# Second sequence's input rows in the first attention: squares turned by VectorE and moved by DMA in place of TensorE transposes

## The chip, the core and the metric

The kernel runs on one core of one Trainium2 chip. The metric is the device time of one execution in microseconds (us), as the median of several runs. A profile is one execution recorded by the hardware; its times are counted from the start of its span.

## The reference, cut to what matters

Two layers, each an attention and a gated feed-forward block with residual and layer norm, on an input x of 2 sequences of 512 rows of 512 numbers, all float32. The change lies in the first attention:

```
q   = x @ Wq.T + bq                    # only 8 of 32 heads of 128 are used
sig = elu(q) + 1
num = einsum('bshd,hde->bshe', sig, M) ;  den = einsum('bshd,hd->bsh', sig, z) + 1e-6
x   = layernorm(x + repeat(num / den, 4 heads) @ Wo.T)
```

The keys and values of this attention do not enter the output, so the kernel leaves them out. The feed-forward block that follows takes weights that are meant to have three values (-s, 0, s); the kernel checks this at run time and has two ways to go on.

## The kernel before, in words

All matmuls contract over the 128 partitions, so x must stand transposed: features on partitions, rows along the free axis. For each of the 2 sequences the first attention keeps such a copy, `xt_a00` and `xt_a01`, 128 x 4 x 512 numbers: four blocks k of 128 features for 512 rows. `query_products` (L323) makes one head of one sequence: four matmuls, one per block k, add up into one PSUM buffer of 128 x 512. `queries` (L352) then has ScalarE compute e = exp (L361) and r = relu (L363) from PSUM, and VectorE q = min(e, 1) + r (L365). The tiles e and r have two buffers each, q has sixteen. There are eight PSUM buffers in all, taken in turn.

The loops stand at L453 to L493. The first sequence's heads 0 to 7 run first. `first_rows` transposes that sequence's rows tile by tile for head 0, so that work starts as rows arrive. In the loop, after head 4, `sum_weights` adds up groups of output weights and `turn_memory` transposes m; after head 6 `transposed(xs[1], "a01")` (L115) makes the second sequence's copy: 16 TensorE transposes (L125) of 128 x 128 into four PSUM buffers, two ScalarE copies and two VectorE copies into `xt_a01` (L127). On TensorE they come to stand before head 7. Then the second sequence's heads follow. Between them stand `fold` (output weights multiplied into m, giving `mw`), and, for the ternary check, `largest` (L177, VectorE: the greatest weight of the first gate/up chunk), `over_partitions` (L184, a TensorE transpose) and `scales` (L195 to L199), which give `inv_up`. From the second sequence's head 3 on, `check_up` has ScalarE divide gate/up chunks by the scale (L433) and VectorE compare them (L204). After that `read` (L392) multiplies the queries by `mw` and adds the result to x.

The order on each engine is set by a scheduling layer from program order and expected readiness, except where `tc.issue_after(step)` ties a step behind another; GpSimd keeps the program's order. Each engine works through its own list in order, and a waiting instruction holds up all behind it. Loads are issued from SyncE's list (SP), a few from ScalarE's; each issue is itself an instruction there. A load signals its landing through one of eight completion semaphores, which loads of both lists take in turn; an issue waits until the load that last used its semaphore has landed.

Loads in order: x of the first sequence, query weights `wq`, x of the second sequence (four tiles `x_1_0` to `x_1_3`, L89), `m`, then 16 output weight tiles `wo` (two per head, L305, pool of six buffers, so that later ones wait for `sum_weights` of earlier ones, L380 and L382), with the first gate/up chunk `gu0` ahead of head 6's, the other ten chunks (L237, 512 KB each), and small weights of the second layer.

`mw` is 128 x 8 x 512; its last column holds z (L321, GpSimd).

Of the kernel before, what the change touches and what calls it, by code (L numbers as in the profile page):

```python
# [10 lines left out]
F32 = mybir.dt.float32  # L11
# [3 lines left out]
AF = mybir.ActivationFunctionType  # L15
ALU = mybir.AluOpType
# [3 lines left out]
P = 128  # L20
B, S, HID = 2, 512, 512
NT = S // P
NK = HID // P
NH, G, D = 8, 4, 128
INTER = 1376
CHUNKS = [(i, min(P, INTER - i)) for i in range(0, INTER, P)]
GROUPS = [4, 4, 3]
LN_EPS = 1e-5
DEN_EPS = 1e-6
LAST = HID - 1  # L30
LENT = 3
TOP12 = -4096
BELOW_HALF = 0.5 - 2.0**-13
# [3 lines left out]
def kernel(  # L37
# [19 lines left out]
    nc = tc.nc  # L57
# [6 lines left out]
    xtp = ctx.enter_context(tc.tile_pool(name="xtp", bufs=2))  # L64
# [7 lines left out]
    wqkv = const.tile([P, NK, 3 * D], F32, tag="wqkv", name="wqkv")  # L72
    bv = const.tile([P, D], F32, tag="bv", name="bv")
    wo1 = const.tile([D, HID], F32, tag="wo1", name="wo1")
    bo = const.tile([P, HID], F32, tag="bo", name="bo")
# [3 lines left out]
    def psum(name):  # L79
        return ps.tile([P, 512], F32, tag="mm", name=name)  # L80


    xs = [[], []]
# [9 lines left out]
    bq = const.tile([D, NH], F32, tag="bq", name="bq")  # L93
    z = const.tile([D, NH], F32, tag="z", name="z")
# [20 lines left out]
    def transposed(rows, name, in_turn=False):  # L115

        xt = xtp.tile([P, NK, S], F32, tag="xt", name=f"xt_{name}")
        done = None
        for k in range(NK):
            pt = psum(f"pt_{name}_{k}")  # L120
            with ExitStack() as tied:
                if in_turn and k:
                    tied.enter_context(tc.issue_after(done.ins))
                for t in range(NT):
                    done = nc.tensor.transpose(pt[:, ts(t, P)], rows[t][:, ts(k, P)], ident)  # L125
            move = nc.vector.tensor_copy if k == 1 or k % 2 > in_turn else nc.scalar.copy
            copies.append(move(xt[:, k, :], pt))  # L127
        return xt
# [43 lines left out]
    def largest(blocks, name):  # L172

        k = len(blocks)
        mx = small.tile([P, k], F32, tag=f"mx{k}", name=f"mx_{name}", bufs=1)
        for i, w in enumerate(blocks):
            nc.vector.reduce_max(mx[:, i : i + 1], w, AX.X)  # L177
        return mx
# [52 lines left out]
    def up_weights(gu_in, name, chunks=range(len(CHUNKS))):  # L231
        gus = []
        for c in chunks:
            i, n = CHUNKS[c]
            gu = wffn.tile([P, 2, NK, n], F32, tag=f"gu{c}", name=f"gu{name}_{c}")
            at = 2 * HID * i
            nc.sync.dma_start(  # L237
                gu.rearrange("p a k i -> p (a k i)"),
                gu_in[at : at + 2 * HID * n].rearrange("(p f) -> p f", p=P),
            )  # L240
            gus.append(gu)
        return gus
# [38 lines left out]
    with tc.tile_pool(name="a0w", bufs=1) as a0w, tc.tile_pool(name="a0", bufs=2) as a0:  # L281
        wq = []
# [16 lines left out]
        for h in range(NH):  # L299
            halves = []  # L300
            if h == 6:
                gus = up_weights(gu0_in, "0", range(1))
# [3 lines left out]
                halves.append(w)  # L306
            wos.append(halves)

        gus += up_weights(gu0_in, "0", range(1, len(CHUNKS)))
        nc.sync.dma_start(wqkv, wqkv_in.rearrange("(k p) f -> p k f", p=P))  # L310
        bqk = const.tile([D, 3], F32, tag="bqk", name="bqk")
        nc.sync.dma_start(bqk, bqk_in)
        nc.sync.dma_start(bv, bv_in.to_broadcast([P, D]))
        nc.sync.dma_start(wo1, wo1_in)
        nc.sync.dma_start(bo, bo_in.to_broadcast([P, HID]))

        mw = a0w.tile([D, NH, HID], F32, tag="mw", name="mw")  # L320
        nc.gpsimd.tensor_copy(mw[:, :, LAST], z)  # L321

        def query_products(pq, xt, h, at):  # L323
            for k in range(NK):
                done = nc.tensor.matmul(  # L325
                    pq[:, at], wq[h][:, k, :], xt[:, k, at],
                    start=(k == 0), stop=(k == NK - 1),
                )
            return done

        def first_rows(xt, t):

            pt = psum(f"pt_a00_{t}")
            for k in range(NK):
                done = nc.tensor.transpose(pt[:, ts(k, P)], xs[0][t][:, ts(k, P)], ident)
            pt = pt.rearrange("p (k t) -> p k t", k=NK)
            nc.scalar.copy(xt[:, :2, ts(t, P)], pt[:, :2])
            nc.vector.tensor_copy(xt[:, 2:, ts(t, P)], pt[:, 2:])
            return done

        def first_queries(pq, xt):
# [7 lines left out]
                    done = query_products(pq, xt, 0, ts(t, P))  # L349
            return done  # L350

        def queries(b, xt, h):  # L352

            pq = psum(f"pq_{b}_{h}")
            if b == h == 0:
                done = first_queries(pq, xt)
            else:
                done = query_products(pq, xt, h, slice(0, S))

            e = a0.tile([D, S], F32, tag="e", name=f"e_{b}_{h}")  # L360
            nc.scalar.activation(e, pq, AF.Exp, bias=bq[:, h : h + 1])  # L361
            r = a0.tile([D, S], F32, tag="r", name=f"r_{b}_{h}")
            nc.scalar.activation(r, pq, AF.Relu, bias=bq[:, h : h + 1])  # L363
            q = a0.tile([D, S], F32, tag="q", name=f"q_{b}_{h}", bufs=16)
            nc.vector.scalar_tensor_tensor(q, e, 1.0, r, ALU.min, ALU.add)  # L365
            qs[b].append(q)
            return done

# [8 lines left out]
        def sum_weights(eng, h):  # L377

            w, w1 = wos[h]
            eng.tensor_add(w, w, w1)  # L380
            s = a0.tile([D, HID], F32, tag="wos", name=f"wos{h}", bufs=4)
            eng.tensor_add(s, w[:, 0, :], w[:, 1, :])  # L382
            wos[h] = s

        def fold(h):
            p = psum(f"pmw_{h}")
            nc.tensor.matmul(p, m[:, h, :], wos[h], start=True, stop=True)
            c = small.tile([P, 1], F32, tag="col", name=f"col_{h}", bufs=2)
            nc.scalar.mul(c, p[:, LAST:], -1.0)
            nc.scalar.activation(mw[:, h, :LAST], p[:, :LAST], AF.Identity, bias=c)  # L390

        def read(b, t, between):  # L392
# [3 lines left out]
            for h0 in range(0, NH, 4):  # L396
                four = []
                den = small.tile([P, 4], F32, tag="den", name=f"den_{b}_{t}_{h0}")
                for j in range(4):
# [5 lines left out]
                    nc.scalar.activation(  # L405
                        den[:, j : j + 1], po[:, LAST:], AF.Identity, bias=den_eps
                    )
                    four.append(po)
                nc.vector.reciprocal(den, den)
                for j in range(4):  # L410
                    d = den[:, j : j + 1]
                    if h0 + j < LENT:
                        y = a0.tile([P, HID], F32, tag="y", name=f"y_{b}_{t}_{j}", bufs=3)
                        nc.scalar.activation(  # L414
                            y[:, :LAST], four[j][:, :LAST], AF.Copy, scale=d
                        )
                        if ys:
                            nc.gpsimd.tensor_add(  # L418
                                ys[0][:, :LAST], ys[0][:, :LAST], y[:, :LAST]
                            )  # L420
# [32 lines left out]
        xt = xtp.tile([P, NK, S], F32, tag="xt", name="xt_a00")  # L453
        with tc.issue_after(queries(0, xt, 0).ins):
            queries(0, xt, 1)
        for h in range(2, NH):
            queries(0, xt, h)
            if h == 4:
                sum_weights(nc.gpsimd, 0)
                turn_memory()  # L460
                sum_weights(nc.vector, 1)
            elif h == 6:
                xt1 = transposed(xs[1], "a01")
                sum_weights(nc.vector, 2)
        sum_weights(nc.gpsimd, 3)
        for h in range(NH):
            queries(1, xt1, h)
            if h == 0:
                sum_weights(nc.vector, 4)
                sum_weights(nc.gpsimd, 5)  # L470
                fold(0)
                fold(1)
                mx_up = largest(
                    [gus[0][:, a].rearrange("p k i -> p (k i)") for a in range(2)], "up"
                )
            elif h == 1:
                top_up = over_partitions(mx_up, "up")
            elif h == 2:
                sc_up, inv_up = scales(top_up, "up")
                fold(2)  # L480
                fold(3)
                sum_weights(nc.vector, 6)
                sum_weights(nc.gpsimd, 7)
            elif h == 3:
                fold(4)
            elif h == 5:
                fold(5)
                fold(6)
            elif h == 6:
                fold(7)  # L490
            if h >= 3:
                for _ in range(3):
                    check_up(*checks.pop(0))  # L493
# [250 lines left out]
    gus = up_weights(gu1_in, "1", range(6, len(CHUNKS) - 1))  # L744
    gus.append(joined_weights(gu1_in, len(CHUNKS) - 1))
    wds = down_weights(wd1_in, "1")
    gus = up_weights(gu1_in, "1", range(6)) + gus
# [91 lines left out]
    for b in range(B):  # L839
# [5 lines left out]
        xt = xt_a1[b]  # L845
# [4 lines left out]
        for j in range(2):  # L850
            p = psum(f"pqk_{b}_{j}")
# [11 lines left out]
        for t in range(NT):  # L863
            p = psum(f"pv_{b}_{t}")
# [167 lines left out]
    t = NT - 1  # L1032
# [248 lines left out]
```

## Time and profile before

| what | value |
|---|---|
| median of 3 runs | 471.82 us (471.29 to 472.02) |
| the profiled execution's own time | 471.99 us |
| its span | 470.0 us |
| mean granted TensorE clock | 0.996 |
| TensorE busy | 463.0 us (99%) |
| VectorE, ScalarE, GpSimd busy | 327.9, 268.1, 114.4 us |
| DMA | 33.97 MB, mean 72 GB/s |
| small DMA packets | 3440 under 512 B, of 15187 |

How to read it: busy time is the sum over an engine's instructions. A matmul that waits for its PSUM buffer or for its operand can be shown as a long matmul, so a busy TensorE isn't TensorE at its peak. The page also has the span in 40 equal slices (each digit is the busy share in tenths), the chain of work that ended last, and groups of instructions by line. In the timeline an entry has its start, its duration, engine, line, output and inputs, and in brackets the idle time before it and what ended it. Names have their buffer numbers left out: `xt_a` is any of the two copies, `pt_a` a PSUM buffer of transposes.

The chain that ended last runs through TensorE for 72% of the span, ScalarE for 7% and VectorE for 5%. Between 54.9 and about 118 us it runs through ScalarE and VectorE, before and after mainly through TensorE.

### The profile page before, as it was taken

The numbers are of one execution on the slowest core, as the hardware profiler recorded it, in microseconds if no ns is written. First come the engines' busy times: TensorE is split into PE (matmuls) and PEld (weight loads), VectorE is DVE, ScalarE is ACT, GpSimd is POOL, SyncE is SP. The second block draws the span as 40 slices with busy tenths as digits, with TensorE's granted clock in tenths as the row PEclk, the third lists the DMA queues.
The fourth block names the chain that finished last, engine by engine and source line by source line (L and its number), as shares of the span: only waits on it lengthen the run. The fifth ranks groups of instructions, "written<-read, shape, count | busy, mean of one in ns | idle before, by whom it ended". The sixth has DMA issues, their size and how long they took to land.

```text
span 470.0 us, 5725 instructions
## 1 busy us (share of the span) xinstructions
PE 463.0 (99%) x1899; PEld 330.7 (70%) x1899; DVE 327.9 (70%) x622; ACT 268.1 (57%) x507; POOL 114.4 (24%) x141
## 2 busy tenths in 40 slices
PE   9999999999999999999999999999999999999995
PEld 8454444434478788888866568888888888888885
DVE  1265677767857677755988989986666767998633
ACT  3344799557556877645756743575644768532201
POOL 0343101566460090400348032000000000041101
PEclk9999999999999999999999999999999999999998
DMA  8999800000015000213192000000000000001011
GB/s 311 373 348 382 301 2 0 0 0 3 1 54 188 3 1 1 92 47 81 58 360 94 0 1 1 1 0 1 1 0 1 0 1 1 1 24 45 22 46 45
DMA packets 15187, 33.97 MB, mean 72 GB/s; under 512 B 3440, under 2 KB 4336, under 8 KB 15152
## 3 DMA queue, kind: packets, MB, share of 16 engines
q1 hardware_dynamic: 14864, 33.14, 19.6%
q8 instruction: 22, 0.36, 0.3%
q10 hardware_dynamic: 288, 0.36, 0.2%
q14 instruction: 13, 0.11, 0.1%
HBM read 31.40 MB, written 2.10 MB: 71 GB/s over the span
## 4 chain that ended last, share of the span: by engine, by line
PE 72%; ACT 7%; DVE 5%; issue 3%; POOL 0%; POOLq 0%; DVEq 0%; ACTq 0%
PE pm L1071 17%; PE pg_f L567 9%; PE pu_f L567 8%; PE pc L1071 8%; PE pdm L1159 7%; PE pd_f L622 4%; PE pdc L1159 4%; DVE x L423 4%; PE pqk L853 3%; PE po L401 2%; ACT y L414 2%; ACT t L433 2%; PE pv L866 2%; PE pot L949 1%; PE po L965 1%
## 5 line engine op out<-in xcount | busy, mean ns | idle before, releaser
L401 PE MATMUL po<-mw,q 128*128 128x512 f32 x128 | 57.1, 598 | 0.3 <-DVE mv_a L137 0.2
L325 PE MATMUL pq<-xt_a,wq 128*128 128x512 f32 (+1 forms) x152 | 56.9, 526 | 0.0
L143 POOL TENSOR_TENSOR rstd_f<-mv_f,ln_eps 128x1 f32<-128x1 f32 x15 | 4.4, 295 | 172.1 <-DVE mv_f L1174 130.2
L401 PEld LDWEIGHTS po<-mw,q 128*128 128x128 f32 x128 | 23.0, 189 | 32.1 <-issue 17.7
L325 PEld LDWEIGHTS pq<-xt_a,wq 128*128 128x128 f32 x152 | 26.2, 190 | 27.3 <-issue 26.2
L1071 PE MATMUL pm<-r,ugu 128*128 128x512 f32 x152 | 37.7, 389 | 0.0
L1071 PE MATMUL pm<-r,it_early 128*128 128x512 f32 x144 | 36.7, 392 | 0.0
L1071 PEld LDWEIGHTS pm<-r,ugu 128*128 128x128 f32 x152 | 28.5, 188 | 5.9
L1071 PEld LDWEIGHTS pm<-r,it_early 128*128 128x128 f32 x144 | 27.0, 188 | 6.0 <-issue 0.5
L423 DVE SCALAR_TENSOR_TENSOR x<-po,den,x 128x511 f32<-128x511 f32 x40 | 29.8, 745 | 1.9
L165 ACT ACTIVATE ta_f<-y_f,below_half 128x512 int8<-128x512 f32 (+1 forms) x22 | 15.9, 723 | 23.7 <-DVE y_f L155 23.3
L1081 DVE SCALAR_TENSOR_TENSOR ev_q<-pm,ev_q 128x512 f32<-128x512 f32 x27 | 18.6, 687 | 14.1 <-PE pm L1071 14.1
L418 POOL TENSOR_TENSOR y<-y,y 128x511 f32<-128x511 f32 x16 | 20.3, 1272 | 31.5 <-ACT y L414 30.8
L593 DVE SCALAR_TENSOR_TENSOR it_f<-tb_f,ta_f 128x512 fp32r<-128x512 int16 (+1 forms) x22 | 15.2, 690 | 16.3 <-ACT tb_f L166 16.3
L361 ACT ACTIVATE e<-pq,bq 128x512 f32<-128x512 f32 x16 | 11.1, 691 | 24.1 <-PE pq L325 21.7
L567 PE MATMUL pg_f<-xh,tu 128*128 128x512 f32 x88 | 24.7, 401 | 0.0
L1080 ACT ACTIVATE ev_q<-pc 128x512 f32<-128x512 f32 x27 | 16.0, 594 | 14.1 <-PE pc L1071 14.0
L435 POOL TENSOR_SCALAR td<-wd,inv_down 128x512 fp32r<-128x512 f32 x11 | 18.6, 1710 | 22.0 <-DVE inv_down L199 22.0
L567 PE MATMUL pg_f<-xl,tu 128*128 128x512 f32 x88 | 23.6, 390 | 0.0
L567 PE MATMUL pu_f<-xh,tu 128*128 128x512 f32 x88 | 23.6, 389 | 0.0
L567 PE MATMUL pu_f<-xl,tu 128*128 128x512 f32 x88 | 23.5, 389 | 0.0
L961 ACT ACTIVATE x<-x,off_f,rstd_f 128x512 f32<-128x512 f32 x7 | 5.7, 816 | 27.7 <-POOL off_f L960 27.7
(310 smaller groups left out, 1088.3 us busy)
## 6 DMA issues: line engine op xcount, KB each, us to landing
gu<-in_gu SPq DMA_DIRECT2D x20, 512.0 KB, 8.0
wo<-in_wo SPq DMA_DIRECT2D x16, 512.0 KB, 5.7
wd<-in_wd SPq DMA_DIRECT2D x20, 256.0 KB, 4.9
wq<-in_wq SPq DMA_DIRECT2D x8, 256.0 KB, 4.1
x<-in_x SPq DMA_DIRECT2D x7, 256.0 KB, 4.4
out<-x SPq DMA_DIRECT2D x7, 256.0 KB, 2.0
wqkv<-in_wqkv SPq DMA_DIRECT2D x1, 768.0 KB, 10.7
m<-in_m SPq DMA_DIRECT2D x1, 512.0 KB, 5.8
```

Of the source, the lines that this page charges most:

```text
L165: nc.scalar.activation(a[:n], y, AF.Relu, bias=below_half[:n])
L325: done = nc.tensor.matmul(pq[:, at], wq[h][:, k, :], xt[:, k, at], start=(k == 0), stop=(k == NK - 1),)
L401: nc.tensor.matmul(po, qs[b][h0 + j][:, ts(t, P)], mw[:, h0 + j, :], start=True, stop=True,)
L418: nc.gpsimd.tensor_add(ys[0][:, :LAST], ys[0][:, :LAST], y[:, :LAST])
L423: steps.append(nc.vector.scalar_tensor_tensor(x[:, :LAST], four[j][:, :LAST], d, x[:, :LAST], ALU.mult, ALU.add))
L435: eng.tensor_scalar(out, w, factor, None, ALU.mult)
L567: nc.tensor.matmul(pp[a], t[:, a, i % NK, :], x2[b][i], start=(i == 0), stop=(i == 2 * NK - 1),)
L622: nc.tensor.matmul(pd, inter[b][c][:, ts(t, P)], td[c].bitcast(F32R), start=(c == 0), stop=(c == last),)
L1071: nc.tensor.matmul(p, w, x, start=(left[id(p)] == begun[id(p)]), stop=(left[id(p)] == 1))
L1080: nc.scalar.activation(ev, pc, AF.Copy, scale=CROSS)
L1081: nc.vector.scalar_tensor_tensor(ev, pm, MAIN, ev, ALU.mult, ALU.add)
L1159: nc.tensor.matmul(p[:, :w], got[j // 4][1][kind][:, j % 4], down_parts[j][kind][:, cols], start=(j == 0 and kind == kinds[0]), stop=(j == ...
```

## The change

The 16 transposes and four copies are gone. `xt_a01` has another layout, 128 x 4 x 4 x 128: tile of rows t, block k, row within the tile. VectorE transposes each of the four tiles of the second sequence's rows in squares of 32 x 32 that stay where they are (`turn_squares`) into the first half of `mw`, which isn't needed yet. The squares are then brought to their places by DMA: 16 transfers inside SBUF on ScalarE's list (`move_squares`), each from 32 partitions to 32 partitions with 16 runs of 32 numbers (128 bytes) per partition, 64 KB in all. The VectorE squares are tied behind q of the first sequence's head 0, and two groups of eight transfers behind r of heads 1 and 2. `query_products` reads the second sequence as four runs of 128 columns. As `mw` is lent out, z is written to it only after the second sequence's head 0. `largest` is tied behind q of the first sequence's head 6. The loads from the second gate/up chunk on are issued from a function that is called later in the program.

```diff
+SQ = 32
-        gus += up_weights(gu0_in, "0", range(1, len(CHUNKS)))
-        nc.sync.dma_start(wqkv, wqkv_in.rearrange("(k p) f -> p k f", p=P))
...
+        def later_loads():
+            gus.extend(up_weights(gu0_in, "0", range(1, len(CHUNKS))))
+            nc.sync.dma_start(wqkv, wqkv_in.rearrange("(k p) f -> p k f", p=P))
...
         mw = a0w.tile([D, NH, HID], F32, tag="mw", name="mw")
-        nc.gpsimd.tensor_copy(mw[:, :, LAST], z)
...
+                rows = xt[:, :, k, :] if xt is xt1 else xt[:, k, at]
                 done = nc.tensor.matmul(
-                    pq[:, at], wq[h][:, k, :], xt[:, k, at],
+                    pq[:, at], wq[h][:, k, :], rows,
...
+        xt1 = xtp.tile([P, NT, NK, P], F32, tag="xt", name="xt_a01")
+        squares = mw[:, :NT, :]
+
+        def turn_squares(t):
+            nc.vector.transpose(squares[:, t, :], xs[1][t])
+
+        def move_squares(i):
+
+            src = squares.rearrange("p t (k i) -> p (t k) i", k=NK)
+            dst = xt1.rearrange("p t k i -> p (t k) i")
+            for j in range(P // SQ):
+                nc.scalar.dma_start(dst[ts(j, SQ), :, ts(i, SQ)], src[ts(i, SQ), :, ts(j, SQ)])
...
+        relus, elus = [], []
...
-            nc.scalar.activation(r, pq, AF.Relu, bias=bq[:, h : h + 1])
+            relus.append(nc.scalar.activation(r, pq, AF.Relu, bias=bq[:, h : h + 1]))
-            nc.vector.scalar_tensor_tensor(q, e, 1.0, r, ALU.min, ALU.add)
+            elus.append(nc.vector.scalar_tensor_tensor(q, e, 1.0, r, ALU.min, ALU.add))
...
         for h in range(2, NH):
             queries(0, xt, h)
+            if h == 2:
+                with tc.issue_after(elus[0].ins):
+                    for t in range(NT):
+                        turn_squares(t)
+            if h < 4:
+                with tc.issue_after(relus[h - 1].ins):
+                    for i in range(2):
+                        move_squares(2 * h - 4 + i)
...
             elif h == 6:
-                xt1 = transposed(xs[1], "a01")
                 sum_weights(nc.vector, 2)
         sum_weights(nc.gpsimd, 3)
+        later_loads()
         for h in range(NH):
             queries(1, xt1, h)
             if h == 0:
+                nc.gpsimd.tensor_copy(mw[:, :, LAST], z)
...
-                mx_up = largest(
-                    [gus[0][:, a].rearrange("p k i -> p (k i)") for a in range(2)], "up"
-                )
+                with tc.issue_after(elus[6].ins):
+                    mx_up = largest(
+                        [gus[0][:, a].rearrange("p k i -> p (k i)") for a in range(2)], "up"
+                    )
```

More of the change, by code (lines that the diff above doesn't have):

```diff
@@ L307 @@
             wos.append(halves)
-        gus += up_weights(gu0_in, "0", range(1, len(CHUNKS)))
-        nc.sync.dma_start(wqkv, wqkv_in.rearrange("(k p) f -> p k f", p=P))
         bqk = const.tile([D, 3], F32, tag="bqk", name="bqk")
[L312 to L315, printed above, removed]
+        def later_loads():
+            gus.extend(up_weights(gu0_in, "0", range(1, len(CHUNKS))))
+            nc.sync.dma_start(wqkv, wqkv_in.rearrange("(k p) f -> p k f", p=P))
+            nc.sync.dma_start(bqk, bqk_in)
+            nc.sync.dma_start(bv, bv_in.to_broadcast([P, D]))
+            nc.sync.dma_start(wo1, wo1_in)
+            nc.sync.dma_start(bo, bo_in.to_broadcast([P, HID]))
         mw = a0w.tile([D, NH, HID], F32, tag="mw", name="mw")
-        nc.gpsimd.tensor_copy(mw[:, :, LAST], z)
         def query_products(pq, xt, h, at):
             for k in range(NK):
+                rows = xt[:, :, k, :] if xt is xt1 else xt[:, k, at]
                 done = nc.tensor.matmul(
-                    pq[:, at], wq[h][:, k, :], xt[:, k, at],
+                    pq[:, at], wq[h][:, k, :], rows,
                     start=(k == 0), stop=(k == NK - 1),
```

## The prediction

> **What bounds the kernel now.** I read the 40 slices of the page, then the timeline of the first 50 us, then busy time by stage, then the DMA views.
>
> The slices (11.75 us each) have TensorE busy throughout, and the DMA engines full for the first five:
>
> ```profile
> PE   9999999999999999999999999999999999999995
> DMA  8999800000015000213192000000000000001011
> GB/s 311 373 348 382 301 2 0 0 0 3 1 54 188 3 1 1 92 47 81 58 360 94 0 1 1 1 0 1 1 0 1 0 1 1 1 24 45 22 46 45
> ```
>
> The timeline around the edited step (start, duration, engine, line, idle time before it):
>
> ```profile
> 30.53 5.82 SPq L305 DMA_DIRECT2D wo<-in_wo  x4
> ...
> 32.18 1.91 PE L125 MATMUL pt_a<-ident,x 128*128 128x128 f32 x16
> ...
> 33.93 7.03 PE L325 MATMUL pq<-xt_a,wq 128*128 128x512 f32 x16
> ...
> 34.75 1.28 DVE L177 TENSOR_REDUCE mx_up<-gu 128x1 f32<-128x512 f32 x2 [1.23 <-DMA gu<-in_gu]
> ...
> 37.56 0.69 ACT L361 ACTIVATE e<-pq,bq 128x512 f32<-128x512 f32 x1 [2.95 <-PE pq L325]
> 37.75 1.21 DVE L380 TENSOR_TENSOR wo<-wo,wo 128x1024 f32<-128x1024 f32 x1
> ...
> 45.95 0.27 PE L184 MATMUL pmx_up<-ident,mx_up 128*2 128x128 f32 x1
> ```
>
> Here TensorE sets the pace: a head takes 7.03 / 2 = 3.5 us, ScalarE and VectorE wait for it, and 16 transposes stand between two heads. Head 7 of the first sequence runs from 33.93, so the second sequence's first head starts at about 37.4; it is the first reader of xt_a01. From 54 us ScalarE is full, so TensorE's "busy" there is mostly waiting for PSUM:
>
> ```profile
> 46.00:54.00 8.00, 8.00 (x22) 3.64 (x21) 4.46 (x9) 5.15 (x10) 2.03 (x2) 1.00 1.03 402
> 54.00:75.00 21.00, 21.00 (x51) 9.28 (x50) 14.82 (x38) 20.78 (x40) 0.00 (x0) 1.00 0.11 37
> ```
>
> (columns: stretch, length, then busy time and instructions of PE, PEld, DVE, ACT, POOL, clock, DMA share, GB/s). ScalarE's weight checks (L433) need inv_up, which comes from TensorE's L184 and L195. So a delay of TensorE before 50 us moves all that follows, one to one; so does a gain, if L184 moves too.
>
> The DMA view of 20 to 40 us, then that of 219 to 226 us, where three loads have rows of 384, 128 and 256 bytes:
>
> ```profile
> DMA packets 1864, 6.79 MB, mean 340 GB/s; under 512 B 206, under 2 KB 206, under 8 KB 1864
> q1 hardware_dynamic: 1864, 6.79, 93.8%
> wo<-in_wo SPq DMA_DIRECT2D x10, 512.0 KB, 5.5
> ```
>
> ```profile
> DMA packets 1585, 0.41 MB, mean 59 GB/s; under 512 B 1584, under 2 KB 1584, under 8 KB 1584
> q1 hardware_dynamic: 1584, 0.39, 27.1%
> gu<-in_gu SPq DMA_DIRECT2D x1, 192.0 KB, 2.7
> gu<-in_gu SPq DMA_DIRECT2D x1, 64.0 KB, 3.9
> ```
>
> The stretch that receives the 16 moves is 94% full. A small packet costs 0.271 x 16 x 7 us / 1584 = 19 ns[...], a 4 KB one, at 400 GB/s over 16 engines, 163 ns.
>
> [...]
>
> **The change, part by part.**
>
> *Removed.* 16 transposes: 33.93 - 32.18 = 1.75 us of TensorE, on the path. Two ScalarE copies (1.07 us) and two VectorE copies (2 x 0.68), both in idle time: worth nothing. TensorE now wants xt_a01 at 37.4 - 1.75 = 35.6.
>
> *VectorE squares.* Four 128x512 transposes; the nearest row, a 128x512 copy, takes 0.68[...]. x_1_3 is issued at 9.0 and lands 5.0 later. VectorE is idle from 12.9 (query 0 of head 0)[...]; I take 15.6, when ScalarE finishes r of head 1 and can issue.
>
> *ScalarE's 16 issues.* 0.41 us is its one such row, 0.51 that of the 512-row load on SyncE: 8 us in all. ScalarE idles 2.17 us per head here, so this alone would be hidden.
>
> *The waits of those issues* decide. The built program has eight completion semaphores, which loads of both queues take in turn, and an issue waits until the last load with its semaphore has landed. Moves 3 to 6 wait for wo0's second, wo1's second, and wo2's two loads; moves 7 to 16 each wait for the move four earlier. The last is at the end of the chain wo1 -> move 4 -> 8 -> 12 -> 16. VectorE's add of wo1 starts at 21.90 in the trace, on its landing: move 4 goes out at 22 at the earliest. Four links then give the arrival of xt_a01: 22 + 4 x link.
>
> *One link.* A lone move of 512 packets takes at least 2.7 and at most 3.9 us to land by the two rows above; I take 3.2, of which 512 x 19 ns / 16 = 0.6 is data. Beside queued weights each engine has 32 rows of a move to serve in turn with 4 KB rows. If a turn is one row: 32 x (163 + 19) ns = 5.8, a link of 3.2 - 0.6 + 5.8 = 8.4 us.[...] I take 7.6[...]. Arrival: 22 + 30.4 = 52.4; bounds 45.2 and 55.6, and 34.8 if no turn is ever lost.
>
> *Cost on the path.* The first head of the second sequence starts at 52.4 instead of 37.4: +15.0, transposes already counted. TensorE has been idle since 35.6[...].
>
> *What is queued behind.* On ScalarE, e and r of heads 3 to 7 and two copies of m stand among and behind the moves: 5 x 1.37 + 1.07 = 7.9 us. Move 16 goes out at 44.8, so they are done by 52.7, before the next head ends at 55.8. TensorE meanwhile fills PSUM buffers of heads 3 to 7 and m, seven of eight: no stall from that. On SyncE, the two loads of wo4 take the semaphores of moves 1 and 2, and three later gate/up chunks those of moves 13 to 15: weights come later, but their readers are later too. On GpSimd, the copy of z into mw waits for the moves that read it and holds the sums of heads 5 and 7, read late in the second sequence: nothing. later_loads swaps one SyncE load: nothing. Reading xt_a01 as four runs of 128 columns: no row shows it. Four separate 128-column matmuls would cost 36 ns more each (8 of them took 1.17 us at 6.14, against 438 / 4 ns), 9 us over 64 matmul records; one instruction has no such restarts and those after 54 us lie under ScalarE's work: I take nothing, bound 3 us before 54.
>
> Sum: +15.0 + 1.7 = 16.7 on the profiled execution's 471.99 us (span 470.0 and 2.0 around it): 488.7; that execution is 0.17 above the median of 471.82. Forecast 488.5.
>
> **Rivals.**
>
> *Moves pass quickly; the maximum is late.* If links cost 3.2 to 3.9, xt_a01 is there at 35 to 38. Then L177 is next: it now stands after head 6's q, and VectorE's order puts the wo6 sum (37.75 in the trace) ahead of q of head 4, which e of head 6 needs, since e has two buffers. Some 12 of the moves, 12 x 0.6 = 7 us of DMA work, come ahead of wo6 and push it from about 37 to 44; then the sum 1.2, q 0.7, e and r 1.4, q 0.7 and L177's 1.3 end at 49, against 45.95 for L184: +3, 475; up to 481 with double the packet cost. For it: transfers inside SBUF may be cheap. Against: the full queue.
>
> *Packets inside SBUF are dearer*, 60 ns: 31 us of all engines, over 500.
>
> *Faster.* Decides if xt_a01 lands before 35.6 and L177 ends before 45.95 - 1.75 = 44.2: then the transposes are pure gain, 470.1. It needs every link under 3.4 us in a stretch that is 94% full, and weights hardly delayed.
>
> **How the numbers follow.** Crawling moves 0.54 (482 to 494: arrival 45.2 to 55.6[...]); quick moves and late maximum 0.30 (474 to 481); dear packets 0.06; no change 0.04; faster 0.06. A measurement of this kernel tells about 0.2% from none. Range 474 to 496: it leaves out the last three cases, and a little of the first. Faster 0.06, same 0.04, slower 0.90.
>
> **What would show it.** Right: TensorE idle before its first second-sequence head, ended by DMA xt_a; to-landing times of moves of 5 us and more while weights are queued; ScalarE idle before moves 7 to 16 on DMA xt_a; the clock below 1 just after the gap. Wrong: moves that land within 3.5 us, TensorE's wait ended by mx_up or by no DMA, or a later stage that gives the delay back.

## The result, and the profile after

The changed kernel takes 490.34 us (median of 6 runs, 489.27 to 492.93) against 471.63 us before in the same session: a ratio of 1.0391, 95% interval 1.0375 to 1.0407. The forecast was 488.5 in a range of 474 to 496. The profiled execution is the slowest of the six (492.93 us, span 490.7), so the profile shows about 2.6 us more than a typical run.

The slices of the page, now 12.27 us each:

```profile
PE   9980399999999999999999999999999999999995
...
PEclk9995599999999999999999999999999999999999
DMA  8999920000000600022229000000000000001011
```

TensorE, busy throughout before, has a hole in slices 3 to 5, its granted clock is at half there (0.50 from 39.0 to 59.5 us), and the DMA engines are busy into a sixth slice (five before). The timeline of that stretch (entries that end in `q` are issues of transfers, standing in that engine's list):

```profile
12.74 2.85 DVE L338 STREAM_TRANSPOSE mw<-x 128x512 f32<-128x512 f32 x4 [0.18 <-DMA x<-in_x]
...
15.62 1.49 ACTq L345 DMA_DIRECT2D xt_a<-mw  x2
...
31.54 14.39 ACTq L345 DMA_DIRECT2D xt_a<-mw  x7
...
46.03 0.69 ACT L379 ACTIVATE e<-pq,bq 128x512 f32<-128x512 f32 x1 [14.69 <-DMA xt_a<-mw]
...
52.43 0.68 DVE L178 TENSOR_REDUCE mx_up<-gu 128x1 f32<-128x512 f32 x1
...
56.58 5.11 PE L328 MATMUL pq<-xt_a,wq 128*128 128x512 f32 x8 [21.14 <-DMA xt_a<-mw]
...
63.25 3.60 PE L328 MATMUL pq<-xt_a,wq 128*128 128x512 f32 x8
```

The squares are ready at 15.6 us. The 16 moves leave ScalarE between 15.6 and 45.1; ScalarE itself stands still behind them, once for 11.3 us and once for 14.7. TensorE has nothing left from 35.4 on and starts the second sequence's first head at 56.58 in place of 37.4. That head takes 5.11 us, a later one 3.60. The maximum (L178) is finished 3.5 us before TensorE starts: it isn't what TensorE waits for.

Busy time by stage (columns as in the prediction):

```profile
35.50:56.50 21.00, 0.00 (x0) 0.00 (x0) 5.09 (x7) 5.71 (x10) 0.15 (x1) 0.58 1.04 330
...
75.00:96.00 21.00, 21.00 (x50) 9.31 (x49) 14.93 (x37) 20.85 (x40) 0.00 (x0) 1.00 0.00 0
```

The second line is the stage with ScalarE full, which stood at 54 to 75 before, with 20.78 us of ScalarE then and 20.85 now. Nothing is given back: the delay of the first head, 56.58 - 37.4 = 19.2, and 1.5 us of slow clock (5.11 - 3.60) make 20.7, and this execution is 492.93 - 471.99 = 20.9 longer.

The DMA view of 15 to 60 us (packets, MB, share of the engines; q1 is SyncE's queue, q10 ScalarE's; a packet of this view is one row, that is one unbroken run of bytes: the 16 moves of 512 rows are 8192 of q10's 8448):

```profile
q1 hardware_dynamic: 3892, 14.00, 89.1%
q10 hardware_dynamic: 8448, 1.05, 15.7%
...
xt_a<-mw ACTq DMA_DIRECT2D x16, 64.0 KB, 8.2
```

A move needs 8.2 us from issue to landing (median; 6.6 to 12.4), although all of them together take a sixth of the engines' time.

### The profile page after: what moved, and what is told of

Its sections match the earlier page's. It is cut to its first block, busy times and chain, and to the rows that moved or that the text cites. A ratio compares the mean times of both kernels' runs of the same rounds, so it can differ in the third digit from the quotient of the medians.

```text
span 490.7 us, 5721 instructions
## 1 busy us (share of the span) xinstructions
PE 462.6 (94%) x1883; PEld 329.2 (67%) x1883; DVE 328.9 (67%) x624; ACT 266.9 (54%) x505; POOL 110.4 (22%) x141
## 4 chain that ended last, share of the span: by engine, by line
PE 69%; ACT 7%; DVE 5%; issue 3%; POOL 0%; POOLq 0%; DVEq 0%; ACTq 0%
PE pm L1099 16%; PE pg_f L595 8%; PE pu_f L595 8%; PE pc L1099 8%; PE pdm L1187 7%; PE pd_f L650 4%; PE pdc L1187 4%; DVE x L441 3%; PE pqk L881 3%; PE po L419 2%; ACT y L432 2%; ACT t L451 2%; PE pv L894 1%; PE pot L977 1%; PE po L993 1%
## 5 line engine op out<-in xcount | busy, mean ns | idle before, releaser
L328 PE MATMUL pq<-xt_a,wq 128*128 128x512 f32 (+1 forms) x152 | 58.4, 537 | 21.2 <-DMA xt_a<-mw 21.1
L423 ACT ACTIVATE den<-po,den_eps 128x1 f32<-128x1 f32 x64 | 14.5, 275 | 12.3 <-PE po L419 12.3
```

What stands on the lines that cost most here:

```text
L328: done = nc.tensor.matmul(pq[:, at], wq[h][:, k, :], rows, start=(k == 0), stop=(k == NK - 1),)
```

## The experiments

The theory was that of the prediction: a move crawls because its small rows take turns with the weights' 4 KB rows. The fixed-time rival: the length of a link is mostly a fixed time of a transfer beside a full queue, or of the chain of semaphores, whatever the rows. The dear-row rival: small rows inside SBUF are dear by themselves. Each experiment starts from the changed kernel. The diffs show the lines that matter most; the rest of an edit is told in words.

### Longer rows

The squares are laid down so that one partition's part of a move is one run of 2 KB: 32 rows in place of 512.

```diff
-                nc.scalar.dma_start(dst[ts(j, SQ), :, ts(i, SQ)], src[ts(i, SQ), :, ts(j, SQ)])
+                nc.scalar.dma_start(dst[ts(j, SQ), i], src[ts(i, SQ), j])
```

> The same 16 moves of 64 KB on ScalarE's queue, with the same squares, but each partition's 16 pieces of 128 bytes now lie one after another on both sides, so that a move is 32 rows of 2 KB instead of 512 of 128 bytes (2 rows per DMA engine instead of 32). Theory (each engine serves one row of each queue in turn): a move beside queued weights loses 2 turns instead of 32 and lands within about 4 us; the last one lands at or before 36 us, TensorE doesn't wait, and the time is 1.7 us below the kernel before, about 470; at worst 472 where the wo6 sum makes the maximum late. Rival A (the chain of four semaphore waits with a fixed cost of 8 us per move, whatever its rows): no change, 490. Rival B (the mere 1 MB of extra traffic in a full stretch): 490 less little.

Measured: 477.16 us, ratio 1.0095 (1.0074 to 1.0116). The short rows were 13 of the 19 us, and the 1 MB of extra traffic, which is the same here, is not what cost them. But the moves still landed 6.1 us after issue (median; 5.0 to 7.7), and TensorE waited 5.7 us:

```profile
41.83 6.65 PE L328 MATMUL pq<-xt_a,wq 128*128 128x512 f32 x8 [5.72 <-DMA wo<-in_wo]
```

(The label names a weight load; the last row of the moves ended at 41.1, the last move landed at 41.7, and this head reads it.) So the theory holds for most of it, and the fixed-time rival for the rest. The 470 that was expected was missed by 7 us.

### Weights in rows of 2 KB

The wo and gu0 weights are stored so that their loads have rows of 2 KB instead of 4 KB.

```diff
-                nc.sync.dma_start(w, wo0_in[h, :, ts(j, G // 2), :])
+                nc.sync.dma_start(w, wo0_in[h, ts(j, G // 2)].rearrange("g p e -> p g e"))
```

> The moves as in the changed kernel; the output weights and the first gate/up chunks come in rows of 2 KB instead of 4 KB (laid out so in DRAM, same bytes, same number of loads). Theory (row by row turns): the turn of a 128-byte row costs 84 + 13 ns instead of 163 + 13, so the first two moves land about 2 to 3 us sooner than the 9.2 us of the changed kernel; the last arrives only about 1 to 3 us sooner, since more of the 16 then meet queued weights: 487 to 490. Rival (turns counted in bytes, or a packet of many rows): the first two moves land as before, 9 us.

Measured: 490.79 us, 1.0406 (1.0364 to 1.0448), no gain. The DMA view of 20 to 22 us, first of the changed kernel, then of this one:

```profile
q1 hardware_dynamic: 216, 0.79, 96.5%
q10 hardware_dynamic: 213, 0.03, 8.7%
```

```profile
q1 hardware_dynamic: 363, 0.69, 95.7%
q10 hardware_dynamic: 350, 0.04, 15.3%
```

Both show as many rows of one queue as of the other, 216 against 213 and 363 against 350, and with shorter weight rows the moves' rows come 1.6 times as fast. Equal counts alone would also fit several rows of each queue at a time. The start times in the changed kernel's trace exclude that: from 19.8 to 22.3 us, 251 of the 265 short rows begin in the last 5 ns of a weight row or as it ends, where 126 would by chance; for the end of another short row it is 159 against 133. So in this stretch a turn was one row.

That was while the weights' queue was full. From 22.5 to 24.5 us, as that queue runs low, 1239 short rows pass beside 111 of the weights' queue:

```profile
q1 hardware_dynamic: 111, 0.39, 67.1%
q10 hardware_dynamic: 1239, 0.15, 50.6%
```

With weight rows of 2 KB the first two moves landed 8.9 and 9.8 us after issue, against 9.6 and 8.9 in the changed kernel. That is the landing which the rival named, though its way of taking turns is excluded; the expectation of 2 to 3 us was wrong, since a move's time is more than its rows' turns. The next view of the changed kernel, 15.6 to 19.6 us, shows another part:

```profile
q1 hardware_dynamic: 425, 1.55, 99.9%
...
xt_a<-mw ACTq DMA_DIRECT2D x3, 64.0 KB, 8.9
```

Three moves are issued in these 4 us, and queue q10 isn't in the list: it moves no row. Beside the full queue the first move waits 4.1 us for its first row (19.69 - 15.62). It is 3.9 us with long rows, and 4.2 with weight rows of 2 KB. With the other queue empty (the seventh move of the kernel with the weights held back, below) it is 1.25.

### The moves on SyncE's queue

```diff
-                nc.scalar.dma_start(dst[ts(j, SQ), :, ts(i, SQ)], src[ts(i, SQ), :, ts(j, SQ)])
+                nc.sync.dma_start(dst[ts(j, SQ), :, ts(i, SQ)], src[ts(i, SQ), :, ts(j, SQ)])
```

> The same 16 moves of 128-byte rows, issued from SyncE's queue behind the output weights and ahead of the second gate/up chunk: one queue, so no turns between queues. Theory: once the weights ahead are through, the moves go at 13 to 19 ns a row, 0.4 to 0.6 us each; all land within about 11 us of the first issue and xt_a01 is there at 47 to 50, 482 to 485. Rival (128-byte rows inside SBUF or each move cost 8 us whatever is beside them): 16 moves in two groups of eight semaphores take 16 us and more, and TensorE starts later than 52. ScalarE waits for no move in either case.

Measured: 490.11 us, 1.0375 (1.0343 to 1.0408), of two runs: the forecast of 482 to 485 was wrong.

```profile
40.25 10.72 SPq L345 DMA_DIRECT2D xt_a<-mw  x15
...
52.83 5.13 PE L328 MATMUL pq<-xt_a,wq 128*128 128x512 f32 x8 [17.53 <-DMA xt_a<-mw]
```

From the seventh on the moves landed in 2.1 us, as short rows (the six before, with loads still ahead of them, in 2.9 to 6.1); what made them late is their place. The scheduling layer put all but one behind wo's last loads, and 15 issues of 0.71 us follow each other from 40.25 on. The dear-row rival falls: alone the short rows aren't slow.

### TensorE kept busy

22 matmuls that nobody reads fill the gap.

```diff
+        warm = psum("warm")
+        for _ in range(22):
+            nc.tensor.matmul(warm, ident, xt[:, 0, :], start=True, stop=True)
```

> The changed kernel with 22 more matmuls of 128x512 on TensorE (into a PSUM buffer that nothing reads) between the first sequence's last head and the second's first, some 19 us in a gap of 21. Theory: the clock stays full through the gap, the second sequence's first head takes 3.4 instead of 5.1 us, the end comes 1.5 to 2 us sooner, 488.5. Rival (the clock in the gap costs nothing, or the first head was slow from its operand's layout): no change, first head 5 us.

Measured: 489.70 us, 1.0363 (1.0340 to 1.0387).

```profile
55.43 3.67 PE L328 MATMUL pq<-xt_a,wq 128*128 128x512 f32 x8 [1.02 <-DMA xt_a<-mw]
```

The first head takes 3.67 us instead of 5.11, so the slow clock costs 1.4 us there. The granted clock is 1.00 from 35.6 to 53.9 us, against 0.59 in the changed kernel, and 1.00 from 56.4 to 75. The gain in the medians, 0.6 us, is within the runs' spread; only the head's time shows it.

### The weights held back

In a first form the loads from wo3 on are tied behind move 16.

```diff
+                with tc.issue_after(moved.ins):
+                    load_wo(range(3, NH))
```

> The change as it is (ScalarE's list, 128-byte rows, the same 16 links and waits), but wo3 to wo7 and gu0 are issued only after move 16 has been issued, so from about 21 us SyncE's queue is empty. Theory (the full queue beside it sets the link): moves that are issued after 21 land in 2 to 3 us, xt_a01 is there at 30 to 32; the weights are some 9 us late and the maximum with them, 472 to 477. Rival (the link's length is the ScalarE queue's own or the chain of semaphores, whatever the other queue does): landings stay at 6 us or more, xt_a01 at 45 or later, 482 or more.

Measured: 490.27 us, 1.0375 (1.0346 to 1.0404), with landings of 8.2 us. This tells nothing of either theory: the tie orders the two in the program, but makes SyncE wait for nothing, and the loads went out beside the moves as before. The second form holds them back by data: GpSimd writes four numbers, read from xt_a01, into wo3's buffer before wo3 is loaded, and the later loads stand behind wo3's.

```diff
+                    if h == 3 and j == 0:
+                        nc.gpsimd.tensor_copy(w[:, 0, :4], xt1[:, 0, 0, ::SQ])
                     load = nc.sync.dma_start(w, wo0_in[h, :, ts(j, G // 2), :])
```

> The change as it is (ScalarE's list, 512 rows of 128 bytes, the same 16 moves), but wo3 to wo7 and all gate/up loads are held back by data: GpSimd first writes four numbers, read from xt_a01, into wo3's buffer, so that these loads wait until every move has landed. Once wo2 has landed (about 21 us) nothing else is on the DMA engines. Theory (the weights beside it set the pace of the moves): moves issued after 21 land in 2 to 3 us, at the 0.7 us of an issue each, and xt_a01 is there at 30 to 33, before TensorE wants it at 35.6; the time goes to the late weights, 476 to 482. Rival (the pace is the ScalarE queue's own, or that of the chain of semaphores): landings stay at 6 us and more and xt_a01 comes after 42, over 484.

Measured: 478.12 us, 1.0135 (1.0108 to 1.0161), within the 476 to 482 of the theory. The DMA view of 26 to 34 us, with nothing else on the engines:

```profile
q10 hardware_dynamic: 5318, 0.66, 49.1%
...
xt_a<-mw ACTq DMA_DIRECT2D x10, 64.0 KB, 2.1
```

Same list, same short rows: a move lands in 2.1 us, where the first six, issued while wo0 to wo2 were still on their way, took 4.1 to 9.2. A row costs 0.491 x 16 x 8 us / 5318 = 12 ns. The last move lands at 33.8, and TensorE goes on without a gap. The waits on semaphores are not quite the same, since no weight load takes one in between and a move then waits for one six to eight earlier, not four; but the time from issue to landing starts after that wait. So ScalarE's queue isn't slow by itself, and it isn't the semaphores that make a link long: weights on the other queue do. What is left is the price of the late weights: TensorE now waits for the maximum (L185, at 45.95 before), and its next head takes 6.10 us in place of 3.60:

```profile
48.24 1.28 DVE L178 TENSOR_REDUCE mx_up<-gu 128x1 f32<-128x512 f32 x2 [1.21 <-DMA gu<-in_gu]
...
49.67 0.37 PE L185 MATMUL pmx_up<-ident,mx_up 128*2 128x128 f32 x1 [4.88 <-DVE mx_up L178]
49.84 6.10 PE L337 MATMUL pq<-xt_a,wq 128*128 128x512 f32 x8
```

### Early on SyncE's list

Here the moves are issued by SyncE between wo2's second load and wo3's first, where SyncE waits for a buffer anyway; first with rows of 2 KB, then with rows of 128 bytes.

```diff
-                with tc.issue_after(relus[h - 1].ins):
-                    for i in range(2):
-                        move_squares(2 * h - 4 + i)
+                for i in range(2):
+                    move_squares(2 * h - 4 + i)
+            if h == 3:
+                load_wo(range(3, NH))
```

> The 16 moves in rows of 2 KB, issued from SyncE's list between wo2's second load (issued at about 12.6 us) and wo3's first, where SyncE otherwise waits until 21.3 for a buffer. Theory (a move is cheap; what makes it slow is standing on a second queue beside a full one, and its place behind other loads): from the end of VectorE's squares at 15.6, 16 issues of 0.7 us end at about 27, landings of about 2 us, xt_a01 there at 28 to 29, TensorE does not wait for it, and the removed 1.75 us of transposes show: 470 to 471. The wo and gu0 loads come about 5 us later, which their readers bear. Rival (a later wait takes over: the maximum L177 or the sums of wo come late by those 5 us): 473 to 476.

> The same place on SyncE's list, but the moves as in the change, 512 rows of 128 bytes. If small rows cost only their 13 ns each when no weights stand beside them (0.42 us a move, under the 0.7 us of its issue), this equals the kernel with long rows: xt_a01 at 28 to 30, 470 to 472. If small rows themselves are what is slow: later than 36, over 475.

Measured: 472.61 us, 1.0015 (1.0003 to 1.0028), with long rows; 474.98, 1.0057 (1.0039 to 1.0075), with short ones. The moves landed in 2.0 and 2.3 us (medians; the first ones, with wo0 to wo2 still ahead of them, took up to 9.1), the last at 31.7 and 34.2. TensorE didn't wait for xt_a01 in either, but the removed 1.75 us doesn't show. Neither reached the 470 to 471 and 470 to 472 that were expected. With long rows:

```profile
15.74 14.52 SPq L352 DMA_DIRECT2D xt_a<-mw  x16
...
44.61 0.27 PE L185 MATMUL pmx_up<-ident,mx_up 128*2 128x128 f32 x1
...
49.72 1.85 DVE L407 TENSOR_TENSOR wos<-wo 128x512 f32<-128x512 f32 x1 [0.70 <-PE pmw L412]
...
51.49 1.76 DVE L390 SCALAR_TENSOR_TENSOR q<-e,r 128x512 f32<-128x512 f32 x1
```

TensorE's L185 is 45.95 - 44.61 = 1.3 us ahead of before. But wo3's load waits until SyncE is through, at 30.4 instead of 21.8 before, and the late weight sums on GpSimd now fall on the start of the ternary check: two VectorE steps beside them take 1.85 and 1.76 us in place of 0.69 (before, one did), and the check's third division on ScalarE starts at 53.95, against 54.07 before. With short rows wo3's load goes out later still, at 32.8, and TensorE waits for the maximum:

```profile
46.77 0.27 PE L185 MATMUL pmx_up<-ident,mx_up 128*2 128x128 f32 x1 [2.68 <-DVE mx_up L178]
```

That the late weights are the cause is read from these two traces, not shown by a run of its own.

### The moves between the weight loads

Ten moves ahead of wo3, the others two by two between the next loads; long rows.

```diff
+                in_order(lambda: nc.sync.dma_start(dst[ts(j, SQ), i], src[ts(i, SQ), j]))
+                if j % 2 == 1:
+                    between()
```

> Rows of 2 KB, moves on SyncE's list: ten of them ahead of wo3's first load, then two behind each of the next three wo loads, so that their issues fill SyncE's idle time without holding the weights back. xt_a01 should be there at 29 to 34, and the weights 2 to 3 us late instead of 9. If it was the late weights (sums of wo on GpSimd and VectorE at the same time as the ternary check) that used up the gain of the kernel with all 16 moves ahead of wo3, the removed 1.75 us shows now: 470 to 471. If not: 472 to 473 again.

Measured: 473.40 us, 1.0035 (1.0020 to 1.0050): the forecast of 470 to 471 was wrong. The moves behind weight loads of their own queue landed behind them (the last six took 4.0 to 6.2 us), and TensorE waited 2.2 us for xt_a01 at 35 us; the slow clock that followed (0.68 in the next head) took 1.8 more.

```profile
37.23 5.37 PE L344 MATMUL pq<-xt_a,wq 128*128 128x512 f32 x8 [2.21 <-DMA xt_a<-mw]
```

### Twelve moves on two lists

Long rows; the four diagonal squares stay on their partitions and are copied by GpSimd, four moves go by ScalarE, eight by SyncE ahead of wo3.

```diff
+            nc.gpsimd.tensor_copy(dst[ts(i, SQ), i], src[ts(i, SQ), i])
+            for n in range(1, P // SQ):
+                j = (i + n) % (P // SQ)
+                eng = nc.scalar if n == 1 else nc.sync
+                eng.dma_start(dst[ts(j, SQ), i], src[ts(i, SQ), j])
```

> An attempt at the best of it: rows of 2 KB; the four squares on the diagonal, which stay on their partitions, are copied by GpSimd (idle until about 19 us), four of the other twelve moves go on ScalarE's list and eight on SyncE's ahead of wo3's first load. SyncE should be through at 23 to 24 us instead of 30.4, so the weights are 2 to 3 us late and xt_a01 is there by about 26. If late weights alone used up the gain of the kernel with all 16 moves ahead of wo3, this gives 470 to 471.3, below the kernel before; if something else did, 472 to 473.

Measured: 471.96 us, 0.9997 (0.9987 to 1.0006), 22 runs from 470.28 to 473.25: no difference that can be told from the kernel before. It lies between the two results that were to decide, so it doesn't decide whether late weights alone use up the gain. In the profiled execution, 470.45, nearly the whole gain stands:

```profile
44.01 0.27 PE L185 MATMUL pmx_up<-ident,mx_up 128*2 128x128 f32 x1
```

That is 1.9 us ahead of before. Why the median has only 0.2 of it stays open; the profile is of one of the quickest runs.

### All but the moves

The squares are turned and not read, the loads and the maximum stand as in the change, TensorE transposes as before.

```diff
-                        move_squares(2 * h - 4 + i)
...
+                xt1 = transposed(xs[1], "a01")
```

> All of the change but the moves: VectorE turns the squares (nobody reads them), z is written late, the maximum is tied behind q of head 6, the later loads come later in the program; the second sequence's rows are turned by TensorE as before. The prediction took all of this at nothing: 471.5 to 472.5. If VectorE's squares or the other ties cost something by themselves, it shows here as more than 473.

Measured: 471.88 us, 0.9993 (0.9985 to 1.0001). VectorE's squares, 0.71 us each here, the late copy of z and the ties cost nothing, as forecast. What this kernel leaves out of the change is the moves and the reading of xt_a01 in four runs; a head takes 3.60 us with either reading, so the loss comes from the moves.

## Why the prediction was right, and where it was off

*What is removed.* TensorE was to want xt_a01 at 35.6; it ran out of work at 56.58 - 21.14 = 35.4. Right.

*Squares and issues.* Squares ready at 15.6, as forecast, at 0.71 us each; the nearest row before, a copy at 0.68, gives the same: 12.9 + 4 x 0.68 = 15.6. An issue took 0.59 us where 0.41 to 0.51 was taken, and was hidden as forecast.

*The waits of the issues decide.* Right. Single issues in the trace: move 4 at 21.6 (forecast 22), 8 at 29.4, 12 at 36.8, 16 at 45.1 (forecast 44.8). Move 4 went out at 21.59, 0.02 us after wo1's second load, the last with its semaphore, had landed; move 8 at 29.39, 0.02 us after move 4.

*One link.* This is the term that was mis-sized. The 7.6 was an estimate of the author's, below the 8.4 that one row a turn gave; so was the link of 5.8 behind the lower bound of 45.2. The links took 7.8, 7.5, 8.3 and, to the start of the head, 11.4 us, a mean of 8.75 against 7.6: 4 x 1.15 = 4.6 us of arrival, less 0.4 from the earlier start, and TensorE started at 56.6 instead of 52.4, in this execution even past the bound of 55.6. Most of the miss is in the last link. The typical run is 2.6 us shorter than the profiled one.

The parts were put together wrongly. A lone move takes 2.1 us, below the 2.7 that was its lower end; its rows 12 ns rather than 19, which was a mean over rows of 128 to 384 bytes. Beside weights, a turn of one row is what the trace shows (216 rows against 213, and 251 of 265 short rows right behind a weight row); the trace before showed no turns, so there it was an assumption. 32 turns of (0.965 x 16 x 2 us / 216 = 143 ns) + 13 ns are 5.0 us. And there is a wait of 4 us before the first row, beside a full queue, which the sum had inside its lone move at some 2.6 us and which the kernel with long rows laid bare. What makes these 4 us isn't settled: halving the weights' rows left them at 4.2.

Nor does 4.1 + 5.0 give a move's time in general. With weight rows of 2 KB the same sum is 4.2 + 32 x (84 + 14 ns) = 7.3 (84 and 14 from its DMA view, in the same way), and the median landing there was 8.5. Turns were lost while the weights' queue was full (96.5% of the engines' time from 20 to 22 us); when it ran low (67.1% from 22.5 to 24.5) the first three moves of the changed kernel landed together, at 25.2, 25.4 and 25.6. So that 7.6 came near the measured links is in part luck: the wait was too short in it, the lone row too dear, and it was put below the turns that it reckoned with.

*Clock.* The 1.7 of the sum was an estimate of the author's: behind its start the trace before has no gap of TensorE over 0.3 us, and its granted clock is 0.996. Measured: 1.5 in the head (5.11 against 3.60, at a granted clock of 0.72), and 1.4 with TensorE kept busy.

*Sum.* 16.7 forecast; 18.7 between the medians, 20.9 in the profiled execution. There the difference of 4.2 is the link.

*What is queued behind.* ScalarE's backlog was done at 51.7 (forecast 52.7), no PSUM stall, no late maximum, nothing from GpSimd; all of this as forecast. A head of four 128-column runs takes 3.60 us, exactly as long as before:

```profile
42.51 3.60 PE L325 MATMUL pq<-xt_a,wq 128*128 128x512 f32 x8
```

One reading of the lines was wrong, though the sum doesn't rest on it: TensorE from 54 to 75 us isn't mostly waiting for PSUM. Its 51 matmuls in 21 us are 0.41 us each, no slower than the 3.5 / 8 = 0.44 of the heads before, so both TensorE and ScalarE are full there.

*Rivals.* Quick moves with a late maximum: not in this kernel, but it is what happens where the weights are held back (478.12; 475 to 481 was worked out) and with short rows early on SyncE's list (474.98). There the weights are late because they stand behind the moves, not because the moves' rows push them. Dear packets of 60 ns: refuted by the 12. Faster: even twelve moves in the best place found give no gain in the median. That transfers inside SBUF may be cheap is borne out only in part. Alone, 512 short rows land in 2.1 us, hardly later than 32 long ones (2.0). But 12 ns for 128 bytes is 2.7 times as much per byte as 143 ns for 4 KB, and it doesn't help where each row has to take its turn with 143 ns of another queue.

## What to carry to other kernels

A small transfer that stood beside a full queue paid here by its number of rows, one turn each while the queue was full (490.34 us with 512 rows a move, 477.16 with 32), and by a wait of 4 us ahead of its first row, not by its bytes: look at what is on the other queue while it runs, and make its rows as long as the layout allows. A move that is cheap by itself (2.1 us to land) still took a place in a list of loads; in a stretch that is 94% full the place was paid for by the weights loaded after it. In none of the places tried here were 1.75 us of transposes on the path worth 12 or 16 transfers.

## What was not expected of the hardware

The cost of TensorE's gap didn't grow with its length. The first head after a gap of 2.2 us took 5.37 us (moves between the loads), after 4.9 us 6.10 (weights held back), after 5.7 us 6.65 (long rows), after 21.1 us 5.11, against 3.60 without a gap; the granted clock was 0.68 in the first of these heads, 0.55 with long rows and 0.72 in the changed kernel. So a short gap cost up to twice as much in clock (3.05 us) as a long one (1.5).

The traces show when the clock was low, not why. It was at half for some 3.5 us with the moves between the loads (0.68 over 5.4 us), 6.8 with long rows (0.93 over 5.7 us, then 0.55 over 6.7) and 20.5 in the changed kernel (39.0 to 59.5 us). It fell 3.6 us after the gap began in the changed kernel and 4.9 with long rows, so not in the order of the gaps' lengths. After the gap of 2.2 us it fell when TensorE was at work again: the granted clock is 1.00 from 35 to 37.2 us, the head starts at 37.23, and a weight load at 37.74 still takes 0.19 us, where one at half clock took 0.34 (long rows). What sets these times was not shown.
